# A two-layer decoder on one core: which side of the value product stands still, and where the row transposes of the routed norm are issued

## Chip, cores and metric

The kernel runs on one core of a Trainium2 chip. The metric is the device time of one execution in microseconds; the median of the runs counts. All matrix work is in float32.

## What is computed

Eight batch entries of 256 tokens with 256 features pass through two layers; each sublayer adds to x. Cut to what matters here, the reference is:

```python
x = x + L0_attn(layernorm(x))            # 16 heads of 16, rotary, full softmax
x = x + L0_xattn(ctx, layernorm(x))      # 16 heads of 16, keys and values are halves of ctx,
                                         # a bias per key and a length mask
x = x + L0_ffn(layernorm(x))             # sinkhorn gates, 8 experts, top tokens per expert
x = x + L1_attn(layernorm(x))            # 16 heads of 16, rotary, causal softmax
x = x + L1_xattn(layernorm(x), ctx)      # 16 heads of 64, one null key and value, layernorm
x = x + L1_ffn(layernorm(x))             # shared and routed experts, one expert per token
# one attention of heads of 16:
attn = softmax(einsum('bhqd,bhkd->bhqk', q, k) / 4)
out  = einsum('bhqk,bhkd->bhqd', attn, v)
```

The change touches the three attentions with heads of 16, and one step of the loop over the attention with heads of 64.

## The kernel before, in words

**Units.** The heads of 16 are worked in 24 units, one for each batch entry and attention: layer 0 takes two entries at a time (two `SelfAttention` units, then two `CrossAttention` units), then come eight causal `SelfAttention` units of layer 1. The loop at L850 runs the units in turn. While unit n is in its `core` (the generator `attention`, L315), the generator `beside(n)` (L820) gives out pieces of `end` of unit n-1 and of `prepare` of unit n+1, spread over the seven yields of the core; `experts_at` adds pieces of the layer 0 experts (`chosen_experts`, L627), which run for two entries at a time. The order of instructions on each engine is drawn up by the tile scheduler from this order and from its own estimate of when operands are ready; nothing in this stage is pinned.

**One attention.** `scores(grp)` (L324) makes, for four heads and each of two key tiles, the transposed scores `st` (keys on partitions, queries along the free side) in one of two PSUM buffers; ScalarE's exp (L343) writes them to `pT`; in the causal layer GpSimd sets the masked part to zero (L346), and the second key tile has only its 128 later queries. `values(grp)` (L360) then multiplies: the values `v_pad`, 2 heads padded to 32 columns each, stand still (64 stationary columns), and the exps of one head move (256 columns, or 128). So `o`, one PSUM buffer, holds the result with heads on partitions; the padding of ones in column 16 (`padded_values`, L289) gives the sum of the exps with it. There are four groups of four heads; after the second and the fourth group `o` is copied to `oT` by VectorE and by ScalarE (L387).

**Rows.** `end` (L482, L554) calls `rows_of` (L390): eight TensorE transposes (`oR`, L396) bring `oT` back to tokens on partitions, two reciprocals (L400) and four products (L402) on VectorE divide by the sums and write `att`. In self-attention `att` is transposed (L283) and multiplied by the output weights (`ao`, L494); in cross-attention it is added to x.

**Values.** `put_values` (L297) writes the values of a token tile into the padded buffer with two copies, on ScalarE in self-attention and on GpSimd in cross-attention. There are two padded buffers, one for even and one for odd entries, set up at the start with zeros and ones (L293, L294).

**Heads of 64.** `null_cross_attention` (L1057) loops over the entries b. In an iteration the heads of entry b are weighted (`stx` L1226, `ox` L1264, `den` L1240), entry b+1 gets its layernorm (`tr<-ident,xn`) and its projections k7, v7 and q7 (each in seven block products, `seven`, L1126), and entry b-1 gets the norm and transposes for the routed experts (`routed_norm` L958, `routed_rows` L968, on the page `tr<-ident,xne` at L283). `routed_norm`'s `xn` and layernorm_T's `xn` share one SBUF buffer. From L1379 on the instructions of TensorE are pinned to the order in which they are written, up to `order.close()` (L1407); `routed_rows` at L1377 comes just ahead of that. For the last entry, b = 7, the order is pinned at L1375, ahead of it.

**Products in two halves.** `product` (L272) issues each product as two, for 64 stationary columns each. In the profile each float32 product shows as two weight loads and two multiplies.

Of the kernel before, what the change touches and what calls it, by code (L numbers as in the profile page):

```python
# [28 lines left out]
F32 = mybir.dt.float32  # L29
# [9 lines left out]
P = 128  # L39
# [116 lines left out]
def plain(  # L156
# [139 lines left out]

    def put_values(engine_copy, v_pad, t, v):  # L297

        for g in range(2):
            engine_copy(  # L300
                v_pad[:, t, :, 3 * g, :HD].rearrange("p (c m) d -> p c m d", c=2),
                v.rearrange("p (c g m d) -> p g c m d", c=2, g=2, m=4)[:, g],
            )

    def masked_queries(work, ps, masks):

# [5 lines left out]
                nc.vector.tensor_scalar(qm[:, m], ps, masks[:, m : m + 1], None, ALU.mult)  # L312
        return qm

    def attention(kT, qm, v_pad, scale, causal, bias):  # L315

        def scores(grp):  # L324
            c, mq = divmod(grp, 2)
            pTs = []
            for kt in range(2):
                q0 = P if causal and kt else 0
                n = S - q0
                st = scp.tile([P, 2, 2, S], F32, tag="sc", name="st")  # L330
                for i in range(2):
                    for g in range(2):
                        rows = slice(64 * g, 64 * g + 64)
                        nc.tensor.matmul(  # L334
                            st[:, g, i, :n],
                            kT[rows, c, bass.ts(kt, P)],
                            qm[rows, 2 * mq + i, c, q0:],
                            start=True,
                            stop=True,
                        )  # L340
                pT = work.tile([P, 2, 2, S], F32, tag="pT", name="pT", bufs=4)
                kb = {} if bias is None else {"bias": bias[:, kt : kt + 1]}
                nc.scalar.activation(pT[:, :, :, :n], st[:, :, :, :n], AF.Exp, scale=scale, **kb)  # L343
                if causal:

                    nc.gpsimd.affine_select(  # L346
                        out=pT[:, :, :, :P],
                        in_=pT[:, :, :, :P],
                        compare_op=ALU.is_ge,
                        fill=0.0,  # L350
                        base=0,
                        pattern=[[0, 2], [0, 2], [1, P]],
                        channel_multiplier=-1,
                    )
                pTs.append(pT)
            return pTs

        oT = work.tile([P, 4, S], F32, tag="oT", name="oT")

        def values(grp, pTs, o):  # L360
            c, mq = divmod(grp, 2)
            for kt in range(2):
                q0 = P if causal and kt else 0
                for g in range(2):
                    for i in range(2):
                        nc.tensor.matmul(  # L366
                            o[64 * i : 64 * i + 64, mq, q0:],
                            v_pad[:, kt, 4 * c + 2 * mq + i, 2 * g : 2 * g + 2, :],
                            pTs[kt][:, g, i, : S - q0],
                            start=kt == 0 and g == 0,  # L370
                            stop=kt == 1 and g == 1,
                            skip_group_check=True,
                        )


        ahead = scores(0)
        yield
        for grp in range(4):
            now = ahead
            if grp % 2 == 0:  # L380
                o = op.tile([P, 2, S], F32, tag="o", name="o")
            if grp + 1 < 4:
                ahead = scores(grp + 1)
                yield
            values(grp, now, o)
            if grp % 2:
                (nc.vector.tensor_copy if grp == 1 else nc.scalar.copy)(oT[:, grp - 1 : grp + 1, :], o)  # L387
            yield oT

    def rows_of(oT, dens):  # L390

# [45 lines left out]
    class SelfAttention:  # L437
# [38 lines left out]
            yield  # L476

        def core(self):
            for self.oT in attention(self.kT, self.qm, self.v_pad, 1.0 / math.sqrt(HD), self.layer == 1, None):
                yield  # L480

        def end(self):  # L482
            b = self.b
            att = rows_of(self.oT, dens[:, 2 * self.layer, 2 * b : 2 * b + 2])
            yield
            attT = transposed(att, work, mm, "xnT")
            yield
            for t in range(2):
                xt = x[:, 2 * b + t, :]
                if self.bias is not None:  # L490
                    nc.gpsimd.tensor_tensor(xt, xt, self.bias[1], ALU.add)
                ps = mm.tile([P, 2 * D], F32, tag="mm", name="ao")[:, :D]
                for c in range(2):
                    product(ps, attT[:, c, bass.ts(t, P)], self.wo[:, c, :], c == 0, c == 1)  # L494
                nc.vector.tensor_tensor(xt, xt, ps, ALU.add)
            yield
# [27 lines left out]
    class CrossAttention:  # L524
# [23 lines left out]
            yield  # L548

        def core(self):  # L550
            for self.oT in attention(self.kT, self.qm, self.v_pad, HD**-0.5, False, kbias[:, self.b, :]):
                yield

        def end(self):  # L554
            b = self.b
            att = rows_of(self.oT, dens[:, 1, 2 * b : 2 * b + 2])
            for t in range(2):
                nc.gpsimd.tensor_tensor(x[:, 2 * b + t, :], x[:, 2 * b + t, :], att[:, t, :], ALU.add)
            yield

    first = ExitStack()
    pads = first.enter_context(tc.tile_pool(name="pads", bufs=1))
    padv = [padded_values(pads, f"padv{i}", engine) for i, engine in enumerate((nc.vector, nc.gpsimd))]
    work = first.enter_context(tc.tile_pool(name="aw", bufs=2))
    banks = ExitStack()
    mm = banks.enter_context(tc.tile_pool(name="amm", bufs=3, space=PSUM))
# [177 lines left out]
            yield  # L744


    units = []
    for b in range(0, B, 2):
        for i in range(2):
            units.append(SelfAttention(b + i, 0, wqkv0, wo0, (turned, offset), padv[i]))  # L750
        for i in range(2):
            units.append(CrossAttention(b + i, padv[i]))
    wqkv1, wo1 = weights("l1_wqkv", 3 * D, None), weights("l1_wo", D, None)
    sin1 = const.tile([P, 2, HD], F32, name="sin1")
    for b in range(B):
        units.append(SelfAttention(b, 1, wqkv1, wo1, None, padv[b % 2]))

    nc8 = XH // 2

# [297 lines left out]
    def null_cross_attention(phase):  # L1057
# [301 lines left out]
        for b in range(B):  # L1359
# [8 lines left out]
            else:  # L1368
# [4 lines left out]
                load_shared(late)  # L1373
                routing_tables(late)
                order.enter_context(tc.manual_schedule(engines={mybir.EngineType.PE}))  # L1375
            if b:
                routed_rows(b - 1, routed_norm(b - 1, work), work)  # L1377
            if more:
                order.enter_context(tc.manual_schedule(engines={mybir.EngineType.PE}))  # L1379
                kT, v, qT = key_room(), value_room(), query_room()  # L1380
                k7 = seven("k7", of_ctx, w_terms(kv_blocks, 0), kT, False)
                v7 = seven("v7", of_ctx, w_terms(kv_blocks, 1), v, True)
                q7 = seven("q7", of_x, w_terms(q_blocks, 0), qT, False)
                next(k7)
                rest()
# [1252 lines left out]
```

## Times and profile before

| what | value |
|---|---|
| median of three runs | 1373.66 us (1373.61 to 1374.96) |
| the profiled execution's own time | 1378.17 us |
| its span, first to last instruction | 1376.4 us |
| instructions | 30783 |
| mean granted TensorE clock | 0.996 |
| TensorE idle before an instruction, longest | 8.2 us (first layernorm), 2.6 and 2.4 us (`qkr`) |
| value products L366 | 1536 multiplies, 103.1 us of weight loads beside them |
| transposes of `oT`, L396 | 192 |
| reciprocal L400 / product L402 / copy L387 on VectorE, each | 248 / 281 / 690 ns |
| copy of `o` on ScalarE (L387) / copy into the padded values, each | 586 / 269 ns |
| exp of 128x1024, each | 1022 ns, with the key bias 1114 ns |

A row of the profile names the line, the engine, the operation, the result and its operands, then the shapes as partitions x elements (for TensorE: stationary rows * columns, then the moving side), the count, the busy time and the mean duration of one, and at the end the idle time of the engine just before such instructions with what ended it. PE is TensorE's multiply, PEld its weight load. In a timeline a row begins with the start and the length of a run of like instructions. Runs on PE overlap in it, because the end of one multiply lies behind the start of the next; the distance from start to start is what a run costs.

### The profile page before, as it was taken

To read this page: it belongs to the slowest core of one execution; us is meant where nothing else is said; L and a number is where in the kernel's file an instruction comes from. 1 tells how busy PE (TensorE), PEld (TensorE's weight loads), DVE (VectorE), ACT (ScalarE), POOL (GpSimd) and SP (SyncE) were. 2 spreads that over 40 slices of the span, in tenths; PEclk is the share of its full clock that TensorE was granted. 3 is DMA by queue.
4 is the path that set the end of the run, shared out by engine and by line. 5 is a ranking of instruction groups with operands and counts; after the bars stand their busy time and mean duration, and the time that the engine had idled before them with its cause. 6 is when DMAs were issued, how large, how long until landed. Compare 5 with 4: busy or idle time off the path is not lost.

```text
span 1376.4 us, 30783 instructions
## 1 busy us (share of the span) xinstructions
PE 1336.3 (97%) x13150; PEld 928.6 (67%) x13150; DVE 546.7 (40%) x1592; ACT 474.4 (34%) x758; POOL 384.3 (28%) x485
## 2 busy tenths in 40 slices
PE   6999999999999999999999999999999999999997
PEld 3666756756766756665767676777767645788874
DVE  5444463563475555344333333233222336322213
ACT  2455444443543433431322323142332312132220
POOL 4322052052033243320324323142432422300003
PEclk9999999999999999999999999999999999999999
DMA  8960000000000005000101010201101111599943
GB/s 306 343 225 16 9 25 9 9 24 2 1 9 1 2 10 183 27 1 16 31 18 33 17 32 17 48 20 29 33 16 33 64 32 63 237 372 400 402 159 120
DMA packets 46929, 116.69 MB, mean 85 GB/s; under 512 B 8272, under 2 KB 30400, under 8 KB 42432
## 3 DMA queue, kind: packets, MB, share of 16 engines
q1 hardware_dynamic: 38912, 92.74, 19.8%
q0 software_dynamic: 5152, 18.89, 3.8%
q10 hardware_dynamic: 2720, 3.02, 0.6%
q8 instruction: 105, 1.72, 0.5%
q14 instruction: 40, 0.33, 0.1%
HBM read 104.00 MB, written 27.93 MB: 96 GB/s over the span
## 4 chain that ended last, share of the span: by engine, by line
PE 81%; DMA 6%; DVE 5%; POOL 4%; issue 1%; ACT 1%; SPq 1%; ACTq 0%; POOLq 0%; DVEq 0%
PE st L334 8%; PE o L366 8%; PE v L274 6%; PE h L274 6%; PE k L274 6%; PE wo L274 5%; PE ox L1264 4%; PE stx L1226 4%; PE out L1626 3%; PE out L1443 3%; PE h L952 3%; PE tr L283 3%; PE qk L274 3%; PE hx L952 3%; PE q L274 2%; PE den L1240 2%
## 5 line engine op out<-in xcount | busy, mean ns | idle before, releaser
L366 PE MATMUL o<-pT,padv 128*64 128x256 f32 (+1 forms) x1536 | 171.6, 365 | 1.1 <-POOL pT L346 1.1
L343 ACT ACTIVATE pT<-st 128x1024 f32<-128x1024 f32 (+1 forms) x128 | 110.6, 916 | 88.1 <-PE st L334 87.3
L366 PEld LDWEIGHTS o<-pT,padv 128*64 128x64 f32 x1536 | 103.1, 137 | 52.8 <-issue 10.2
L334 PE MATMUL st<-qm,kT 64*128 64x256 f32 (+1 forms) x1024 | 116.6, 366 | 0.8 <-DVE qm L312 0.6
L334 PEld LDWEIGHTS st<-qm,kT 64*128 64x128 f32 x1024 | 89.4, 188 | 25.9 <-issue 15.6
L1232 POOL TENSOR_TENSOR both<-pTx 128x512 f32<-128x512 f32 x64 | 79.7, 1273 | 46.4 <-ACT pTx L1230 38.9
L274 PE MATMUL h<-xrT,w 128*64 128x128 f32 (+1 forms) x1936 | 87.2, 250 | 0.0
L274 PEld LDWEIGHTS h<-xrT,w 128*64 128x64 f32 x1936 | 84.7, 137 | 2.8 <-ACT yr L1635 1.0
L343 ACT ACTIVATE pT<-st,kbias 128x1024 f32<-128x1024 f32 x64 | 68.0, 1113 | 28.7 <-PE st L334 28.7
L1230 ACT ACTIVATE pTx<-stx 128x1024 f32<-128x1024 f32 x64 | 62.2, 1022 | 41.7 <-PE stx L1226 39.8
L256 POOL TENSOR_TENSOR lnrs<-lnve,mhalf 128x2 f32<-128x2 f32 x48 | 33.7, 704 | 147.5 <-DVE lnve L254 94.4
L334 PE MATMUL st<-qm,memk 64*128 64x256 f32 x512 | 68.8, 393 | 0.5
L945 DVE TENSOR_TENSOR midr<-sl,h 128x128 f32<-128x128 f32 x102 | 29.4, 288 | 100.4 <-PE h L274 67.2
L944 ACT ACTIVATE sl<-h 128x128 f32<-128x128 f32 (+1 forms) x114 | 35.4, 310 | 97.8 <-PE h L274 55.3
L1226 PE MATMUL stx<-qTx,kTx 64*128 64x256 f32 x512 | 64.3, 391 | 2.5 <-ACT pTx L1230 2.5
L274 PE MATMUL qk<-l_wqkv,xnT 128*64 128x512 f32 x256 | 63.0, 613 | 0.7 <-ACT xnT L286 0.7
L346 POOL TENSOR_SCALAR_AFFINE_SELECT pT<-pT 128x512 f32<-128x512 f32 x64 | 40.0, 646 | 81.9 <-ACT pT L343 78.7
L1264 PE MATMUL ox<-pTx,vx 128*64 128x256 f32 x512 | 61.1, 381 | 0.0
L1226 PEld LDWEIGHTS stx<-qTx,kTx 64*128 64x128 f32 x512 | 46.1, 186 | 20.3 <-ACT pTx L1230 7.2
L334 PEld LDWEIGHTS st<-qm,memk 64*128 64x128 f32 x512 | 48.0, 186 | 15.1 <-issue 5.1
L274 PE MATMUL wo<-wout_x,oT 128*64 128x256 f32 x512 | 58.0, 379 | 0.0
L1315 POOL TENSOR_TENSOR oT<-oT,rs 128x512 f32<-128x512 f32 x30 | 37.3, 1275 | 64.8 <-DMA rs<-rd 64.8
(341 smaller groups left out, 2289.5 us busy)
## 6 DMA issues: line engine op xcount, KB each, us to landing
w<-packs SPq DMA_DIRECT2D x22, 1408.0 KB
w<-packs SPq DMA_DIRECT2D x22, 768.0 KB
rs<-rd SPq DMA_DIRECT2D x16, 512.0 KB
packs<-L_ffn_w_eDF SPq DMA_DIRECT2D x8, 704.0 KB
packs<-L_ffn_w_eDF SPq DMA_DIRECT2D x8, 640.0 KB
packs<-L_ffn_w_eFD SPq DMA_DIRECT2D x8, 640.0 KB
ctxT<-ctx_T SPq DMA_DIRECT2D x8, 512.0 KB
wkv_x<-L_xattn_Wkv POOLq DMA_DIRECT2D x1, 4096.0 KB
```

Source lines behind the costliest of these rows:

```text
L274: nc.tensor.matmul(out[h], lhsT[:, h], rhs, start=start, stop=stop, skip_group_check=True)
L283: nc.tensor.transpose(ps[:, c, t * P : (t + 1) * P], rows[:, t, c * P : (c + 1) * P], ident)
L334: nc.tensor.matmul(st[:, g, i, :n], kT[rows, c, bass.ts(kt, P)], qm[rows, 2 * mq + i, c, q0:], start=True, stop=True,)
L343: nc.scalar.activation(pT[:, :, :, :n], st[:, :, :, :n], AF.Exp, scale=scale, **kb)
L366: nc.tensor.matmul(o[64 * i : 64 * i + 64, mq, q0:], v_pad[:, kt, 4 * c + 2 * mq + i, 2 * g : 2 * g + 2, :], pTs[kt][:, g, i, : S - q0], s ...
L952: nc.tensor.matmul(h, shared["ws13"][:, c, lo : lo + P], shared["xnT"][:, c, bass.ts(q, 2 * S)], start=c == 0, stop=c == 1)
L1226: nc.tensor.matmul(st[:, g, kt, :], kT[rows, c, bass.ts(kt, P)], qT[rows, c, :], start=True, stop=True)
L1230: nc.scalar.activation(pT, st, AF.Exp, scale=scale)
L1232: nc.gpsimd.tensor_tensor(both, pT[:, :, 0, :], pT[:, :, 1, :], ALU.add)
L1264: nc.tensor.matmul(o[XD * g : XD * (g + 1), i, :], v[:, kt, 2 * (c2 + i) + g, :], pT[:, g, kt, :], start=kt == 0, stop=kt == 1, skip_group ...
L1443: nc.tensor.matmul(ps, mid[:, i, lo : lo + P], w2[:, i, :], start=i == 0, stop=i == NFC - 1)
L1626: nc.tensor.matmul(ps[h], mid[:, i, h], sets[k % len(sets)][1][:, i, :], start=i == 0, stop=i == NFC - 1, skip_group_check=True,)
```

## The change

It has two parts.

**Exp stands still.** For entries from the third on (b of 2 and more in layer 0) and for all of layer 1, the values lie in new buffers `valv` of 17 columns a head (16 values and a one), and `attention` sees this from the shape. `turned_values` takes the exps of 64 queries as the stationary side (64 columns) and the 17 columns of one head as the moving side. The result has queries on partitions: `o` is 2 token tiles x 8 heads x 17. `weighted` then takes the reciprocals of column 16 and multiplies straight from PSUM into `att`, on VectorE, after the second and fourth group. No `oT` and no `rows_of` are made for these units; `end` finds `att` ready. `put_values` needs one copy a token tile instead of two. Entries 0 and 1 of layer 0 keep the old form.

**Pinned rows.** In the loop over the entries of the attention with heads of 64, the pinned order of TensorE starts ahead of `routed_rows` instead of after it, for b of 1 to 6 (for b = 0 there is no such call).

```diff
     def put_values(engine_copy, v_pad, t, v):
+        if len(v_pad.shape) == 4:
+            engine_copy(v_pad[:, t, :, :HD], v.rearrange("p (h d) -> p h d", d=HD))
+            return
         for g in range(2):
...
+    def values_and_ones(pool, name, engine):
+        t = pool.tile([P, 2, H, HD + 1], F32, name=name)
+        engine.memset(t[:, :, :, HD:], 1.0)
+        return t
...
-    def attention(kT, qm, v_pad, scale, causal, bias):
+    def attention(kT, qm, v_pad, scale, causal, bias, dens):
...
-        oT = work.tile([P, 4, S], F32, tag="oT", name="oT")
+        turned = len(v_pad.shape) == 4
+        if turned:
+            att = work.tile([P, 2, D], F32, tag="att", name="att")
+        else:
+            oT = work.tile([P, 4, S], F32, tag="oT", name="oT")
+
+        def turned_values(grp, pTs, o):
+            c, mq = divmod(grp, 2)
+            for g in range(2):
+                for i in range(2):
+                    head = 4 * g + 2 * mq + i
+                    for t in range(2):
+                        kts = 1 if causal and t == 0 else 2
+                        for kt in range(kts):
+                            for h in range(2):
+                                q = t * P + 64 * h - (P if causal and kt else 0)
+                                nc.tensor.matmul(
+                                    o[64 * h : 64 * h + 64, t, head, :],
+                                    pTs[kt][:, g, i, q : q + 64],
+                                    v_pad[:, kt, 8 * c + head, :],
+                                    start=kt == 0,
+                                    stop=kt == kts - 1,
+                                    skip_group_check=True,
+                                )
+
+        def weighted(c, o):
+            r = dens[:, :, 8 * c : 8 * c + 8]
+            nc.vector.reciprocal(r, o[:, :, :, HD])
+            nc.vector.tensor_tensor(
+                att[:, :, c * P : (c + 1) * P].rearrange("p t (h d) -> p t h d", d=HD),
+                o[:, :, :, :HD],
+                r.unsqueeze(3).to_broadcast([P, 2, 8, HD]),
+                ALU.mult,
+            )
...
             if grp % 2 == 0:
-                o = op.tile([P, 2, S], F32, tag="o", name="o")
+                o = op.tile([P, 2, 8, HD + 1] if turned else [P, 2, S], F32, tag="o", name="o")
...
-            values(grp, now, o)
+            (turned_values if turned else values)(grp, now, o)
             if grp % 2:
-                (nc.vector.tensor_copy if grp == 1 else nc.scalar.copy)(oT[:, grp - 1 : grp + 1, :], o)
-            yield oT
+                if turned:
+                    weighted(grp // 2, o)
+                else:
+                    (nc.vector.tensor_copy if grp == 1 else nc.scalar.copy)(oT[:, grp - 1 : grp + 1, :], o)
+            yield (lambda: att) if turned else lambda: rows_of(oT, dens)
...
         def end(self):
             b = self.b
-            att = rows_of(self.oT, dens[:, 2 * self.layer, 2 * b : 2 * b + 2])
+            att = self.rows()
             yield
...
+    valv = [values_and_ones(pads, f"valv{i}", engine) for i, engine in enumerate((nc.vector, nc.gpsimd))]
...
     for b in range(0, B, 2):
+        padv = padv if b < 2 else valv
...
-        units.append(SelfAttention(b, 1, wqkv1, wo1, None, padv[b % 2]))
+        units.append(SelfAttention(b, 1, wqkv1, wo1, None, valv[b % 2]))
...
+            if more:
+                order.enter_context(tc.manual_schedule(engines={mybir.EngineType.PE}))
             if b:
                 routed_rows(b - 1, routed_norm(b - 1, work), work)
             if more:
-                order.enter_context(tc.manual_schedule(engines={mybir.EngineType.PE}))
                 kT, v, qT = key_room(), value_room(), query_room()
```

## The prediction

> **What bounds the kernel now.** I read the page first (busy shares and the chain), then the PE groups kept apart by shape, then the PE timeline of single stretches, and last the waits of PE.
>
> ```profile
> span 1376.4 us, 30783 instructions
> ...
> PE 1336.3 (97%) x13150; PEld 928.6 (67%) x13150; DVE 546.7 (40%) x1592; ACT 474.4 (34%) x758; POOL 384.3 (28%) x485
> ...
> PE 81%; DMA 6%; DVE 5%; POOL 4%; issue 1%; ACT 1%; SPq 1%; ACTq 0%; POOLq 0%; DVEq 0%
> ```
>
> TensorE sets the time: 97% busy, 81% of the chain. In the waits of PE the whole run holds some 33 us of idle, 8.2 of it the start; between 60 and 660 us, where the changed units lie, it is under 12 us. So the change is priced on PE, by start-to-start distances in its timeline, because a busy sum counts the 0.2 us end of a pipelined run twice.
>
> ```profile
> L366 PE MATMUL o<-pT,padv 128*64 128x256 f32 x1280 | 157.8, 384 | 1.1 <-POOL pT L346 1.1
> ...
> L396 PE MATMUL oR<-ident,oT 128*128 128x128 f32 x192 | 27.1, 280 | 0.5 <-ACT oT L387 0.4
> ...
> L366 PE MATMUL o<-pT,padv 128*64 128x128 f32 x256 | 19.8, 273 | 0.0
> ```
>
> Each float32 product shows as two load-and-multiply pairs. L366 is the value product (64 stationary columns, 256 or 128 moving); L396 turns its result back into rows, 8 transposes in each of 24 units. The next fence has the nearest rows to the new shape: `lg` (8 moving columns) and `cs` (16), both with 64 stationary columns that alternate between the two halves of the output, exactly the order of the new loop.
>
> ```profile
> 144.16 1.95 PE L274 MATMUL ao<-l_wo,xnT 128*64 128x256 f32 x16
> 145.94 0.59 PE L274 MATMUL lg<-gate,xnT 128*64 128x8 f32 x16
> 146.37 1.93 PE L366 MATMUL o<-pT,padv 128*64 128x256 f32 x16
> 148.13 0.36 PE L274 MATMUL cs<-g,ones 128*64 128x16 f32 x8
> 148.42 2.00 PE L334 MATMUL st<-qm,kT 64*128 64x256 f32 x16
> ```
>
> 16 pairs of `lg` take 146.37 - 145.94 = 0.43 us: **26.9 ns a pair**. `cs` between two stages of its own kind (272.48 to 272.68, 8 pairs) takes 25.0. The longest run of such pairs, `h` with 64 moving columns (1214.17 to 1219.31, 176 pairs), takes 29.2.
>
> [...]a 16-instruction L366 group takes 1.76 us before a stage of its own mode and 1.86 before a transpose (139.79 to 141.65), so a change costs some 0.1 us here.
>
> **The change, part by part.** 20 of the 24 units change: 12 in layer 0 (256 queries against two key tiles, 4 groups each: 48 groups) and 8 causal ones (32 groups).
>
> *Transposes out of rows_of.* 8 per unit, as here:
>
> ```profile
> 548.19 1.52 PE L366 MATMUL o<-pT,padv 128*64 128x256 f32 x16
> 549.64 1.58 PE L334 MATMUL st<-qm,kT 64*128 64x256 f32 x16
> 551.15 1.09 PE L396 MATMUL oR<-ident,oT 128*128 128x128 f32 x8
> 552.25 1.58 PE L334 MATMUL st<-qm,kT 64*128 64x256 f32 x16
> ```
>
> 1.10 us here, 1.02 at 262.59, 0.93 at 135.33: mean 1.04, times 20 = **-20.8 us**.
>
> *The value product.* Old, pure stream: 16 instructions in 1.73 us (205.80 to 207.53, 108 ns each); causal, 8 of these and 8 at 54.5 (`h` at 128 columns: 4.85 us for 88, rounded down) = 1.30. Sum 48 x 1.73 + 32 x 1.30 = 124.6 us. New: 32 products, 64 pairs a group, causal 24 and 48: 48 x 64 + 32 x 48 = 4608 pairs. **Break-even is 27.0 ns a pair**; each ns more costs 4.6 us. The bounds are 25.0 (4608 x 0.025 = 115.2: -9.4) and 29.2 (134.6: +10.0). I take 27.5, just over `lg`, because a group is four times as long as `lg`'s run: 126.7, **+2.1 us**. Mode changes at the ends stay as they are.
>
> *The row work.* DVE loses a 0.69 us copy, two 0.25 reciprocals and four 0.28 products per unit (2.3 us) and gets two reciprocals at 0.25 and two products of 256 elements, estimated at 0.48 from the row of `ys` (L736): 1.5. ACT loses a 0.59 copy and, in self-attention, half of its four 0.27 copies into padv; POOL likewise. All of it lies beside PE: nothing gained. What is late next: `o` has one buffer, so the next value product waits for `weighted` (0.73 us, against 0.69 for the old copy), and a score stage of 1.5 to 1.9 us covers that. Without this cover it would be 0.8 us twice a unit. The last unit has no cover: values end at 614.55, transposes of att start at 616.45 over copy, oR, reciprocal and product; now 0.9 us. **-1.0 us.** The two extra memsets of ones (0.09 and 0.14 us by L294) lie in the 8.2 us wait for the input.
>
> *A stall that the transposes covered.* At 549.64 to 553.75 oR parts two score stages. The score buffers are two, so the second stage may not begin before the first exp is done: where two such stages meet elsewhere (stx at 959.32) exp starts 1.24 us in and takes 0.97, and the second stage starts at 2.31 instead of 1.93. In the causal units the stage is only 1.51 long: a stall of 2.25 - 1.51 = 0.74 at most. Upper end 8 x 0.74 + 12 x 0.3 = 9.5 us, lower end 0, since the att transposes (ready by then) can move into the gap. I take 0.1 a unit: **+2.0 us**. The stationary side is now pT, so a whole group needs both exps at its first head, where the old loop needed the second halfway; a score stage lies in between, counted in the same bounds.
>
> *Rows in the pinned order.* For b of 1 to 6 the four xne transposes come before k7's first product instead of inside it:
>
> ```profile
> 977.42 0.66 PE L283 MATMUL tr<-ident,xn 128*128 128x128 f32 x4
> 978.00 0.87 PE L274 MATMUL k<-ctxT,wkv_x 128*64 128x128 f32 x10
> 978.81 0.44 PE L283 MATMUL tr<-ident,xne 128*128 128x128 f32 x2
> 979.17 0.44 PE L274 MATMUL k<-ctxT,wkv_x 128*64 128x128 f32 x4
> ```
>
> That saves three or four mode changes. But xne shares a buffer with xn, so DVE makes it only after PE has read xn: at 978.19 to 978.92, behind a copy of oT that ends at 978.2. The transposes can then end at about 979.2, and k's 31 instructions at 54.5 ns end at 981.0; they now end at 980.84. Queued behind the wait are all of k7, v7 and q7, and the exps of the next entry behind those. +0.15 x 6 = **+0.9 us**; from -0.6 x 6 = -3.6, if DVE makes xne before that copy, to +0.6 x 6 = +3.6, if no mode change is saved.
>
> **Sum.** -20.8 + 2.1 - 1.0 + 2.0 + 0.9 = -16.8 us. The profiled execution took 1378.2 (span 1376.4 and 1.8 around it), so 1361.4 profiled. The runs' median, 1373.66, lies 4.5 under the profiled one: **1356.9**.
>
> **Rivals.** (A) *The pair pitch is longer than lg's.* Place: the 80 changed value groups. It decides from 124.6 + 16.8 + 2.1 = 143.5 us, 31 ns a pair. For it: `sc`, also 8 columns, needs 0.55 us for 16 (1017.49 to 1018.04), 34.4 ns, and no run as long with 17 columns is in the trace; the instruction stream of a group grows fourfold. Against it: 176 pairs at 29.2. At 34.4: 158.5 - 124.6 = +33.9 in place of +2.1: 1388.7, slower. (B) *The gap closes but PE waits.* The transposes were filler; the full score stall (+7.5 over my value) and one more stall like that at 303 (2.44 us, after which y took 3.41 instead of 1.97: the granted clock was 0.72 from 306 to 312[...]) give 7.5 + 3.9: 1368.3. For it: waits of 2.6 and 2.4 us on qkr exist. Against it: stx waited only 2.5 us in all. (C) *Pitch of 30.5 to 31:* +14 to +16 more than my value, 1371 to 1373, no change.
>
> **Numbers.** The forecast's case 0.72, B 0.14, C 0.05, A 0.09. About 0.2% (2.7 us) is what a measurement of this kernel can tell from no change. The pitch bounds alone give 1345.4 to 1364.8; with the stall's upper end, up to B, 1345 to 1368.5, which leaves out A, C and little else. Faster 0.86, same 0.05, slower 0.09.
>
> **What would show it.** Value groups of 64 pairs that follow each other at 1.7 to 1.9 us (causal 1.3 to 1.4); 32 of 192 oR instructions left; PE idle from 60 to 660 us not over 15 us; xne transposes in one run of four after xn's, with a wait of about 0.6 us on DVE. Groups of 2.1 us or more would mean A; a row of waits of st on pT would mean B.

## Result and the profile after

| | before | after |
|---|---|---|
| median | 1374.31 us (1373.61 to 1376.04, 4 runs) | **1391.47 us** (1384.71 to 1397.77, 4 runs) |
| ratio, 95% interval | | **1.0113** [1.0089, 1.0138] |
| span of the profiled execution | 1376.4 us | 1385.7 us |
| first product after the changed stage (`fm`, L274) starts at | 621.1 us | 629.4 us |

The forecast was 1356.9 us, faster; the changed kernel is 17 us slower. The page of the changed kernel, in the order in which I read the one before:

```profile
span 1385.7 us, 36933 instructions
...
PE 1332.5 (96%) x16318; PEld 954.8 (69%) x16318; DVE 528.8 (38%) x1533; ACT 461.7 (33%) x710; POOL 381.3 (28%) x474
...
PE 66%; issue 2%; DVE 2%; POOL 1%; ACT 1%; DMA 1%; SPq 0%; ACTq 0%; POOLq 0%
...
L385 PE MATMUL o<-valv,pT 128*64 128x17 f32 x4608 | 147.3, 210 | 2.4 <-POOL pT L357 2.4
```

TensorE is as busy as before. The new product has the 4608 pairs that were counted on. The transposes went too: 32 of 192 `oR` instructions are left.

```profile
L443 PE MATMUL oR<-ident,oT x32: 272/273/328, 50.8 to 113.2; 128*128 128x128 f32 x32
```

The loss lies in the attention stage (8.3 of the 9.3 us by which the spans differ); an iteration of the loop over the heads of 64 went from 60.61 to 60.73 us. So I looked for it in the timeline of PE. Here it is from 231 us on (start, length of the run, line, operation, shapes, count):

```profile
231.23 1.03 PE L274 MATMUL v<-l_wqkv,xnT 128*64 128x256 f32 x8
232.19 2.00 PE L345 MATMUL st<-qm,kT 64*128 64x256 f32 x16
234.12 0.66 PE L283 MATMUL tr<-ident,qkr 128*128 128x128 f32 x4
234.62 0.60 PE L521 MATMUL qps<-ident,qkr 128*128 128x128 f32 x4
235.15 3.97 PE L385 MATMUL o<-valv,pT 128*64 128x17 f32 x128
239.04 3.58 PE L345 MATMUL st<-qm,kT 64*128 64x256 f32 x16
242.55 0.66 PE L283 MATMUL tr<-ident,xnb 128*128 128x128 f32 x4
243.14 2.00 PE L345 MATMUL st<-qm,kT 64*128 64x256 f32 x16
```

Three score stages `st`, of the same 16 instructions. Those at 232.19 and 243.14 take 1.93 us from start to start; the one at 239.04 takes 3.51. No wait stands ahead of it: no row carries an idle time in brackets. What differs is what ran just before, 128 pairs with 17 moving columns. The same stretch in windows (third column of numbers: the granted clock of TensorE):

```profile
228.00:235.00 7.00, 7.00 (x98) 1.00 0.00 0
235.00:238.50 3.50, 3.50 (x118) 1.00 0.02 5
238.90:242.30 3.40, 3.40 (x22) 0.50 0.26 82
242.30:249.30 7.00, 7.00 (x118) 1.00 0.00 0
```

PE was busy in every microsecond, and still the clock went to half from 238.86 to 242.27, 3.41 us. The execution has three more falls in this stage, at 505, 604 and 624.5 us; these follow waits of 2.2, 2.1 and 1.5 us (the last in two parts, 0.82 and 0.68). So neither waits nor groups of few columns stand ahead of every fall (see "Open" below). The page's `PEclk` row shows none of it: its 40 slices are 35 us long. The waits of PE grew as well; these are the ones that were absent or shorter before (us in total, times, longest):

```profile
PE st L345 <- ACT pT L354: 6.7, 10, 2.1
...
PE cps L737 <- DMA by_half<-slots: 2.8, 2, 2.0
...
PE cs L274 <- DVE g L707: 2.5, 7, 0.8
PE o L385 <- POOL pT L357: 2.4, 2, 2.2
```

To keep the parts apart I use a **ledger of the stage** from 60 us to the start of `fm`, one profiled execution for each kernel. *Clock lost* is the sum over windows of 1 us of (1 - granted clock); *idle* is PE's; *rest* is what remains (an idle microsecond at half clock is taken off twice, a small amount). *Changes* counts, in the order in which TensorE's multiplies start, from the first one to `fm`, how often the rows and columns of the stationary side change (64*128 for scores, 128*128 for transposes, 128*32 for experts, 128*64 for most others).

| kernel | moving columns | changes | `fm` starts | clock lost | idle | rest |
|---|---|---|---|---|---|---|
| before | 256 | 296 | 621.1 | 1.7 | 13.0 | 546.4 |
| after | 17 | 308 | 629.4 | 6.8 | 21.5 | 541.1 |
| values_only | 17 | 308 | 641.5 | 25.6 | 17.5 | 538.4 |
| layer1_only | 17 in layer 1 | 300 | 635.7 | 13.6 | 18.5 | 543.6 |
| no_transposes | 256 | 282 | 606.6 | 0.0 | 17.9 | 528.7 |
| before_late | 256 | 360 | 638.7 | 1.7 | 14.6 | 562.4 |
| late | 17 | 332 | 634.2 | 15.6 | 15.2 | 543.4 |
| late_wide32 | 32 | 318 | 617.0 | 3.4 | 12.8 | 540.8 |
| wide20 | 20 | 311 | 636.1 | 13.7 | 21.3 | 541.1 |
| wide24 | 24 | 308 | 620.2 | 3.4 | 16.9 | 539.9 |
| wide28 | 28 | 284 | 624.1 | 8.6 | 21.2 | 534.3 |
| wide32 | 32 | 282 | 613.0 | 3.4 | 16.0 | 533.6 |
| pinned17 | 17 | 266 | 643.2 | 32.7 | 26.4 | 524.1 |
| pinned24 | 24 | 267 | 625.5 | 10.2 | 26.3 | 529.0 |
| pinned32 | 32 | 267 | 623.2 | 10.2 | 25.0 | 528.0 |
| pinned_before | 256 | 286 | 627.6 | 6.8 | 20.5 | 540.3 |

Some expectations below name counts of changes that differ from these (289, 291 and 293); the table has those of the traces.

The profiled execution of after was one of its quicker ones. Over its four runs (clock 0.990, 0.979, 0.982, 0.991) the time times (1 - clock) is 20.2 us on average; over the 18 runs of before that were timed beside wide24 it is 7.9.

### The profile page after: what moved, and what is told of

It reads as the page before. It is cut to its first block, busy times and chain, and to the rows that moved or that the text cites. A ratio compares the mean times of both kernels' runs of the same rounds, so it can differ in the third digit from the quotient of the medians.

```text
span 1385.7 us, 36933 instructions
## 1 busy us (share of the span) xinstructions
PE 1332.5 (96%) x16318; PEld 954.8 (69%) x16318; DVE 528.8 (38%) x1533; ACT 461.7 (33%) x710; POOL 381.3 (28%) x474
## 4 chain that ended last, share of the span: by engine, by line
PE 66%; issue 2%; DVE 2%; POOL 1%; ACT 1%; DMA 1%; SPq 0%; ACTq 0%; POOLq 0%
PE h L274 6%; PE v L274 5%; PE k L274 5%; PE o L385 5%; PE st L345 4%; PE ox L1316 4%; PE wo L274 4%; PE stx L1278 4%; PE out L1679 3%; PE out L1496 3%; PE h L1004 3%; PE hx L1004 3%; PE q L274 2%; PE den L1292 2%; PE qk L274 2%
## 5 line engine op out<-in xcount | busy, mean ns | idle before, releaser
L385 PEld LDWEIGHTS o<-valv,pT 128*64 128x64 f32 x4608 | 141.5, 138 | 13.9 <-issue 8.7
L385 PE MATMUL o<-valv,pT 128*64 128x17 f32 x4608 | 147.3, 210 | 2.4 <-POOL pT L357 2.4
L345 PE MATMUL st<-qm,kT 64*128 64x256 f32 (+1 forms) x1024 | 121.6, 373 | 5.5 <-ACT pT L354 5.0
L345 PEld LDWEIGHTS st<-qm,kT 64*128 64x128 f32 x1024 | 92.7, 192 | 29.2 <-issue 12.5
L274 PE MATMUL h<-xrT,w 128*64 128x128 f32 (+1 forms) x1936 | 87.3, 250 | 3.9 <-issue 3.9
L274 PEld LDWEIGHTS h<-xrT,w 128*64 128x64 f32 x1936 | 84.7, 137 | 6.8 <-issue 4.6
L345 PE MATMUL st<-qm,memk 64*128 64x256 f32 x512 | 72.3, 396 | 1.9 <-ACT pT L354 1.7
L997 DVE TENSOR_TENSOR midr<-sl,h 128x128 f32<-128x128 f32 x102 | 29.4, 288 | 104.9 <-PE h L274 70.3
L274 PE MATMUL qk<-l_wqkv,xnT 128*64 128x512 f32 x256 | 63.2, 616 | 0.7 <-ACT xnT L286 0.7
L274 PE MATMUL wo<-wout_x,oT 128*64 128x256 f32 x512 | 58.0, 379 | 0.0
```

What stands on the lines that cost most here:

```text
L274: nc.tensor.matmul(out[h], lhsT[:, h], rhs, start=start, stop=stop, skip_group_check=True)
L345: nc.tensor.matmul(st[:, g, i, :n], kT[rows, c, bass.ts(kt, P)], qm[rows, 2 * mq + i, c, q0:], start=True, stop=True,)
L385: nc.tensor.matmul(o[64 * h : 64 * h + 64, t, head, :], pTs[kt][:, g, i, q : q + 64], v_pad[:, kt, 8 * c + head, :], start=kt == 0, stop=k ...
```

## The experiments

Two theories, guesses of mine to be tested. **G**: the granted clock goes by how much streams through the array, not by whether PE is busy; long stretches of products with few columns bring half clock with no wait at all. **W** (the rival): only waits lower the clock, so the loss is the score stall and its like. Later a third joined, **O**: the order that the scheduler draws up.

**1. The product alone.** At the end of the kernel before, stretches of 640 pairs with 64 stationary columns in alternating halves, between full-length products; then 320 pairs with 128 stationary columns.

```python
for i in range(count):
    for h in range(P // m):
        nc.tensor.matmul(ps[m * h : m * h + m, ...], x[:, i % NT, m * h : m * h + m], x[:, i % NT, D - n :], ...)
```

> The kernel before, with six runs of products put in between the attention with heads of 64 and the experts, nothing else changed; the results of the added products are not used. Each run is parted from the next by 48 products with 512 moving columns. 640 pairs each with 64 stationary columns and 17, 32, 64 and 8 moving ones, then 320 pairs each with 128 stationary columns and 17 and 64 moving ones. Theory G [...]: in the 17 and 8 column runs the granted clock falls to 0.5 after at most 7 us and stays there to the end of the run (pitch then 29 growing to 45 or more ns), in the 64 column run it stays at 1.0; 32 shows on which side of the threshold it lies. Theory W (only waits of TensorE lower the clock): the clock is 1.0 in all runs. Pitch: if the issue of the pair is the limit, 17, 32 and 64 columns all give 29 to 30 ns and 8 too; if lg's 26.9 ns was the true value for few columns, 8 and 17 give 27 and 64 gives 29.

Windows of the stretches: 17 columns (cut where the clock falls), 32, 64, 8, then 128 stationary columns with 17 and with 64 moving.

```profile
1173.04:1179.30 6.26, 6.26 (x218) 1.00 0.02 5
1179.30:1201.89 22.59, 22.59 (x430) 0.50 0.01 2
1224.89:1243.52 18.63, 18.63 (x642) 1.00 0.02 4
1264.15:1282.82 18.67, 18.67 (x643) 1.00 0.02 4
1303.42:1332.83 29.41, 29.41 (x642) 0.60 0.01 3
1355.31:1419.21 63.90, 63.90 (x322) 0.54 0.00 1
1442.88:1478.75 35.87, 35.87 (x322) 1.00 0.00 1
```

Nothing waits anywhere here. With 17 columns the full clock lasts 6.3 us and then it is half to the end: 640 pairs take 28.85 us. With 32 or 64 columns the same number takes 18.63 and 18.67 us, 29.1 ns a pair, at full clock throughout. So more work in the same instructions is quicker. With 8 columns the clock falls too (0.60 in the mean), and with 128 stationary columns it falls for 17 moving ones (0.54) and not for 64 (1.00). The half clock without a wait that G expected is there; W's "only waits" does not hold in a bare stretch.

**2. What the pair pitch is, and from how many columns on.**

> As the first probe, with other runs: 640 pairs with 64 stationary columns that alternate between the halves and 20, 24 and 28 moving columns; 320 pairs with 40 moving columns all in one half; 640 pairs with 48 moving columns and the order 0, 0, 1, 1 of the halves. The results of the added products are not used. Theory G: the threshold lies between 17 columns (clock 0.5 in the first probe) and 32 (clock 1.0), so at least one of the three shows the fall and those above it none. Pitch: if two weight loads of 64 columns go on at once, one in each half, the one-half run takes twice the pitch, 56 to 59 ns, and 0, 0, 1, 1 lies between 29 and 58; if the issue of instructions were the limit, all of them would take 29 ns.

20, 24 and 28 columns: 18.64 us for 640 each, the time of 32 columns at full clock (18.63). That none of the three loses the clock was not expected: in a bare stretch of 640 pairs 17 columns lost it and 20 kept it. One half alone, 40 columns: 319 pairs in 18.53 us, **58.1 ns** a pair. Halves in the order 0, 0, 1, 1: 29.1 ns again. So load and multiply take 58.1 ns in one half and, with both halves in turn, half of that: 58.1 / 2 = 29.1, as if the two halves went on side by side. At full clock the pitch stays at 29 ns from 17 to 64 moving columns and is 112 ns with 128 stationary ones (35.87 us for 320): in these runs it goes by the stationary columns and their halves, and not by the moving columns or the number of instructions. `lg` has the same pitch: in its run the starts come in twos, 6 or 7 ns apart, and from two to two it is 58.4 ns, 29.2 a pair. Only the first step from two to two is shorter (28 ns), and over 16 pairs that gives 26.9.

**3 and 4. One part of the change alone.** values_only is after with the pinned order at its old place; pin_only is before with the pinned order moved.

```diff
+            if more:
+                order.enter_context(tc.manual_schedule(engines={mybir.EngineType.PE}))
             if b:
                 routed_rows(b - 1, routed_norm(b - 1, work), work)
             if more:
-                order.enter_context(tc.manual_schedule(engines={mybir.EngineType.PE}))
```

> The changed kernel with the pinned order starting where it did before; only the exps stand still. Both theories: the pinned rows cost 0.1 us in each of six iterations, so 0.5 to 1 us faster than the changed kernel with the same clock; against the kernel before still slower by 0.5 to 1.5%. A time below 1374 us would mean that the pinned rows are the loss.

> The kernel before with only the pinned order moved ahead of routed_rows. Both theories: +0.6 to +1 us against the kernel before (0.1 to 0.15 in each of six iterations), no change in the granted clock; a wait of about 0.6 us on xne's transposes in each iteration.

values_only 1392.61 us against 1377.84, ratio 1.0093 [1.0073, 1.0114]; pin_only 1378.96, ratio 1.0000 [0.9988, 1.0012]. The loss comes with the first part of the change; the pinned rows make no difference that these runs can show. In values_only's profiled execution 25.6 us of clock are lost, in after's 6.8, though TensorE has the same instructions in the same order up to `fm`: the loss is large and changes from execution to execution. Five of the seven falls in values_only's stage (37.5 of its 51.2 us at half clock) have no wait of 0.3 us or more in the 10 us ahead of them. Here is the first one, and the stretch ahead of it:

```profile
155.70:165.90 10.20, 10.20 (x58) 0.50 0.09 27
145.00:155.60 10.60, 10.39 (x256) 1.00 0.01 2
```

**5. More columns, the same instructions.** After, with 32 moving columns: 17 of the head and 15 of its neighbour, whose results nobody reads.

```diff
-                                    v_pad[:, kt, 8 * c + head, :],
+                                    flat_of[id(v_pad)][:, 17 * (16 * kt + 8 * c + head) : 17 * (16 * kt + 8 * c + head) + 32],
...
-                o = op.tile([P, 2, 8, HD + 1] if turned else [P, 2, S], F32, tag="o", name="o")
+                o = op.tile([P, 2, 8, 32] if turned else [P, 2, S], F32, tag="o", name="o")
```

> The changed kernel, but 32 columns move instead of 17: the 17 of the head and the first 15 of its neighbour, whose products land in unused columns of the result. The number of instructions is the same. Theory G: more streams through the array in the value groups (the profile's value group of 64 pairs keeps 1.88 us[...]), the lost clock shrinks and so does the spread of the runs: 1378 to 1385 us. Theory W: the clock and the spread stay as they were (1385 to 1398 us) or the time grows with the columns.

1373.16 us, ratio **0.9963** [0.9950, 0.9976]: quicker than both kernels, and quicker than G's range. The waits that W blames are still there (same columns):

```profile
PE st L350 <- ACT pT L359: 6.8, 10, 2.2
...
PE cs L274 <- DVE g L712: 2.6, 7, 0.6
```

6.8 us in 10 waits of `st`, as in after (6.7 in 10). W falls as the main cause of the lost clock. But not all of this gain is the clock: over its six runs 12.4 us are lost to it, against 20.2 in after, so 7.8 us of the 18 between the two kernels (see 13 to 18).

**6 to 8. Another order.** If long unbroken stretches of value pairs were the trouble, the fourth value group of a unit could go behind the first score stage of the next unit; this would also cover the score stall. late has it with 17 columns, late_wide32 with 32, before_late is the kernel before with it.

```diff
-        for i, _ in enumerate(u.core()):
+        core = u.core()
+        for i in range(7):
+            next(core)
+            if i == 0 and tail is not None:
+                for _ in tail:
+                    pass
...
+        tail = core
+        next(experts_at, None)
```

> The changed kernel (17 columns), but the fourth value group of a unit is issued after the first score stage of the next unit, so that no two value groups follow each other and the score stages have a value group between them. Theory G: no run of value products is longer than 2 us, [...]the clock returns to 0.993 to 0.997, the spread of the runs to that of the kernel before, and the waits of st on pT (6.5 us) fall under 2 us: 1362 to 1372 us. Theory W with the waits alone as the cause: the waits fall too, and the clock with them, but then the 128-pair runs would be innocent, and the widened kernel's clock could not have risen with its waits unchanged.

> The same order with 32 moving columns. Theory G: 1361 to 1370 us; at most 3 us below the 17 columns, since the clock has little left to recover. If the 17 columns lose clock in this order as well, the difference is 5 us or more.

> The kernel before (values stand still, 256 columns move) with this order of the fourth value group. Theory G: its runs of value products stream all the time, so the order gains nothing there by the clock; the score stages had the transposes between them: within 0.3% of the kernel before. If the order by itself is worth 6 us or more, the gain of the late kernel is not due to the clock and the covered stalls of the turned form.

late: 1392.25 us, ratio 1.0129 [1.0106, 1.0152], expectation missed. The clock still falls, at 183, 285 and 371 to 388 us among others, so parting the last two groups of a unit is not enough. late_wide32: 1370.52, ratio 0.9965 [0.9952, 0.9978]: the waits of `st` on `pT` go from 6.8 to 2.0 us, and the time stays, since the rest grows by 7.2. It is 21.7 us quicker than late, and over the runs late loses 17.4 us more to the clock (24.8 and 7.4). before_late: 1391.26, ratio 1.0120 [1.0099, 1.0141], expectation missed too, and the ledger says why: no more clock lost, hardly more idle, but 64 more changes of tile kind and 16.0 us more rest, by estimate **0.25 us a change** (16.0 / 64). The kernels of the table in which all 20 units are turned agree with it: from 266 to 332 changes their rest grows by 0.27 us a change (a straight line through the eleven). I had priced a change at 0.1.

**9. 20 columns in the kernel.**

> The changed kernel with 20 moving columns instead of 17. In the bounds probe 20 columns kept the full clock and 17 lost it, at the same 29.1 ns a pair. Theory G: the full gain of the 32 columns is there already, 1370 to 1376 us, 0.2 to 0.5% under the kernel before[...]. Theory W: as the changed kernel, 1385 us or more.

1395.3 us, ratio 1.0125 [1.0107, 1.0143], missed, with 23.4 us of clock lost over the runs: 20 columns keep the clock in a bare stretch but not here, where transposes, small products and waits lie between the groups.

**10. No transposes, old product.** Before, without the 20 x 8 transposes: `att` is made of the rows of `oT` as they lie and a constant in place of the sums' reciprocals.

```diff
-            for k in range(4):
-                nc.tensor.transpose(ps[:, k, :], oT[:, k, bass.ts(t, P)], ident)
...
+            if through:
...
+            else:
+                rows = oT.rearrange("p k s -> p (k s)")[:, 4 * P * t : 4 * P * (t + 1)].rearrange("p (n w) -> p n w", w=HP)
```

> The kernel before without the eight row transposes in 20 of the 24 units: the products of the row step read oT itself and a constant in place of the reciprocals, so this attention is left out of the result but for its timing. Nothing else changes, and the exps still move. Theory G with the covered stall: the 20.8 us of the transposes come off PE, 3 to 8 us come back as waits of st on pT and of the small chains, the clock stays at 0.994 or more: 1357 to 1366 us. If the whole 20.8 us are gained, 1354 to 1356, the transposes covered nothing and the waits of the changed kernel come from its value product.

1362.57 us against 1379.55, ratio 0.9888 [0.9868, 0.9908], 15.4 us less by the ratio. The stall appears here as well, without a turned product:

```profile
PE st L335 <- ACT pT L344: 6.8, 7, 1.6
```

So the transposes did cover a score stall, and of the 21 us in them some 5 come back as waits (idle 17.9 against 13.0).

**11. Only layer 1 turned.**

```diff
-        padv = padv if b < 2 else valv
```

> The changed kernel with the exps standing still in layer 1 alone (17 columns); layer 0 keeps the old form throughout. Theory G: in layer 1 the runs are 48 pairs (1.4 us) with products of 512 and 256 columns between most of them, so little clock is lost there (at most 4 us); 8 units times 1.04 for the transposes against 8 x 4 x 0.09 for the pitch and up to 0.9 a unit for the stall: -6 to +4, 1369 to 1379 us, and most of the changed kernel's loss is in layer 0. If it is 1384 us or more, layer 1 carries the loss.

1390.64 us, ratio 1.0081 [1.0059, 1.0102], missed. The 8 causal units alone bring most of the loss. Its falls of the clock at 507 and 610 us follow waits of 3.0 us (`o` on the masked `pT`) and 2.1 us (`st` on `pT`); the longest, from 473 to 484 us, has only waits of 0.8 and 0.2 us ahead of it, among groups of 17 columns.

**12. The last wait of wide32.** Its clock falls once more at 587 us, after a wait of 2.2 us in the last unit. wide32_tables makes the tables of the null key after that unit's core.

> The 32-column kernel, and the tables for the null key made after the last unit's core instead of before it, so that their products of 3.6 us lie in the last unit's end chain (waits of 0.8, 0.7 and 0.9 us, and the half clock after them) and their use of pT's buffers no longer holds up that unit's exps (2.2 us). Both theories: 3 to 6 us under the 32-column kernel, 1364 to 1370 us, 0.6 to 0.9% under the kernel before.

1373.34 us, ratio 0.9955 [0.9938, 0.9973], not told apart from wide32's; the expected 3 to 6 us aren't there. The idle went to `nvw` (3.0 us), and the clock falls at 603 instead.

**13 and 14. 24 and 28 columns.**

> The changed kernel with 24 moving columns instead of 17 (7 of the neighbour's, whose results nobody reads). 20 columns still lost the clock in the kernel and 32 did not. [...]the value groups with 24 columns stand between: a ratio to the kernel before between 0.997 and 1.010 and lost clock of 4 to 10 us. If there is a threshold in the kernel just over 20, it is as good as 32: 0.9963 within 0.002, lost clock about 3 us. If the gain with 32 columns came from something else than the streamed amount, 24 is like 20 and 17: 1.011 to 1.013.

> As with 24, with 28 moving columns. Streamed amount: as good as 32 or nearly, 0.996 to 0.999, lost clock 3 to 5 us. Something that belongs to 32 alone: 1.008 or more.

wide24 1382.31 us against 1377.25, ratio 1.0040 [1.0019, 1.0061]; wide28 1376.89, ratio 0.9998 [0.9987, 1.0009]. With 17, 20, 24, 28 and 32 columns the ratios are 1.0113, 1.0125, 1.0040, 0.9998, 0.9963: graded. But wide28 loses as much clock over its runs as wide24 (13.1 and 11.8 us on average; 3 to 5 were expected) and is 5 us quicker, so something else moves along. The order shows it: with 17, 20 and 24 columns there are 308 to 311 changes, with 28 and 32 columns 284 and 282. Only the number of moving columns and the room for them were edited, so the scheduler must have gone by it, presumably through its estimate of how long an instruction takes. Experiment 5 had not held the order fixed.

**15 to 18. One order for all.** TensorE pinned to the written order through all 24 units. With 17, 24 and 32 columns its instructions then stand in the same order up to `fm` (in the trace of 17 columns one transpose in the last unit has another place).

```diff
+    pinned = ExitStack()
+    pinned.enter_context(tc.manual_schedule(engines={mybir.EngineType.PE}))
     for n, u in enumerate(units):
...
+    pinned.close()
```

> The changed kernel with TensorE's instructions of the attention stage (all 24 units) held to the order in which they are written, so that the order no longer hangs on the scheduler's estimates of how long 17 or 32 columns take. If the missing streamed columns cost the clock and the clock is the main loss, this one is slower than the same order with 32 columns by 10 us or more. If most of the difference between 17 and 32 columns was the order (the 32-column kernel has 282 changes of kind among its TensorE runs, the changed kernel 293), this one and the 32-column one lie within 4 us of each other. Against the kernel before: 1.004 to 1.015 by the clock, 0.994 to 0.999 by the order.

> The same order with 24 moving columns. By the clock: between the two others. By the order: equal to both within 3 us.

> The same order with 32 moving columns; written order has 267 changes of kind instead of 282. [...]more waits, since the written order doesn't know what is ready: 0.990 to 1.000 of the kernel before.

> The kernel before with its attention stage in the written order too, to see what the written order does without the change. It has 289 changes of kind instead of 291: 0.995 to 1.010 of the kernel before. If it lies below 0.995, part of what a pinned changed kernel gains is the written order and not the change.

| kernel | median | ratio to before (1377.29 us) | mean clock over the runs |
|---|---|---|---|
| pinned17 | 1397.34 us | 1.0129 [1.0100, 1.0158] | 0.975 |
| pinned24 | 1384.17 us | 1.0049 [1.0032, 1.0065] | 0.984 |
| pinned32 | 1381.31 us | 1.0035 [1.0022, 1.0048] | 0.988 |
| pinned_before | 1383.42 us | 1.0041 [1.0028, 1.0054] | 0.991 |

With one order, 17 columns in place of 32 cost 16.0 us by the medians. In the profiled executions `fm` starts 20.0 us later (643.2 and 623.2), and the clock lost differs by 22.5 (32.7 and 10.2); over all runs it differs by 17.8 (34.7 and 16.9). With instructions, order and waits alike, only the moving columns are left to explain it: G holds as far as these runs go. The two timelines from 150 us on, first pinned17:

```profile
150.88 2.02 PE L385 MATMUL o<-valv,pT 128*64 128x17 f32 x64
153.23 0.41 PE L274 MATMUL cs<-g,ones 128*64 128x16 f32 x8 [0.33 <-DVE g L707]
153.46 2.70 PE L385 MATMUL o<-valv,pT 128*64 128x17 f32 x64
155.94 0.65 PE L274 MATMUL cs<-g,ones 128*64 128x16 f32 x8
156.51 3.79 PE L345 MATMUL st<-qm,memk 64*128 64x256 f32 x16
```

and pinned32, the same five runs:

```profile
151.55 2.04 PE L390 MATMUL o<-valv,pT 128*64 128x32 f32 x64
153.91 0.41 PE L274 MATMUL cs<-g,ones 128*64 128x16 f32 x8 [0.32 <-DVE g L712]
154.13 2.07 PE L390 MATMUL o<-valv,pT 128*64 128x32 f32 x64
156.00 0.42 PE L274 MATMUL cs<-g,ones 128*64 128x16 f32 x8
156.35 2.00 PE L350 MATMUL st<-qm,memk 64*128 64x256 f32 x16
```

The same wait (0.33 and 0.32 us), the same instructions; but the second value group takes 2.48 us instead of 1.87 and the score stage doubles. Windows of 150 to 162 us, pinned17 and then pinned32:

```profile
150.00:162.00 12.00, 11.67 (x188) 0.72 0.08 25
```

```profile
150.00:162.00 12.00, 11.61 (x228) 1.00 0.08 25
```

The order counts too. pinned17 to pinned32 have the lowest rest of all (524.1 to 529.0), but the most idle (25 to 26 us): the written order doesn't know what is ready. pinned32 was expected at 0.990 to 1.000 and missed that. But pinned_before is slower than before, so a pinned kernel is to be held against that one: 1381.31 against 1383.42 us. wide32 stays among the quickest, with late_wide32 and wide32_tables.

## Why the prediction was wrong, step by step

**Transposes, -20.8: right.** The start-to-start sum of `oR` from 110 us to the end of the stage went from 23.6 to 1.0 us; 1.4 of it was idle, so -21.2. (The three distances of the prediction have the mean 1.02 and not 1.04.)

**The value product, +2.1: the step that failed.** Its size, in a layer 0 group with the same stage behind it, before and after:

```profile
287.91 1.95 PE L366 MATMUL o<-pT,padv 128*64 128x256 f32 x16
289.68 1.89 PE L274 MATMUL qk<-l_wqkv,xnT 128*64 128x512 f32 x8
```

```profile
192.60 2.05 PE L385 MATMUL o<-valv,pT 128*64 128x17 f32 x64
194.48 1.92 PE L274 MATMUL qk<-l_wqkv,xnT 128*64 128x512 f32 x8
```

A group of 64 pairs takes 1.88 us, 29.4 ns a pair and not 27.5, against 1.77 for the old one; a causal group takes 1.42 (541.96 to 543.38) against 1.36 (537.47 to 538.83). 48 x 0.11 + 32 x 0.06 = 7.2; all distances of `o` from 115 us on, less idle and half clock, went from 131.9 to 139.3, **+7.4**. Both sides of the sum were off. The old price of 1.73 came from the row at 205.80, which is `back`, of the same shapes but not a value product. And I had taken the price of a pair from `lg`, whose 26.9 ns hold one short step (28 ns in place of 58.4) in so few pairs; the longer runs of probe_bounds gave 58.1 ns in one half and 29.1 in halves by turns. Nor was 25.0 a lower bound: `cs`'s 25.0 has the same short first step as `lg`'s 26.9 (29 and 28 ns), and single starts lie 6 or 7 ns apart. The bound that I had from the long run of `h`, 29.2, was the better neighbour.

More than its size, its **frame** was wrong: I priced the product by its pitch alone, with the clock held at 1, and brought the clock in only under rival B, behind waits. The traces show the clock at 0.50 for 3.41 us or a multiple of it, and not behind waits alone: in probe_pitch 17 columns every 29 ns leave PE at 100% busy, and after 6.3 us the clock falls. Over the runs this is 20.2 - 7.9 = **+12.3 us**, which no step of mine had.

**Score stall and other waits, +2.0:** idle in the stage rose by **8.5** (21.5 - 13.0). The sign, the place (`st` on `pT`, 6.7 us in 10 waits) and the upper end of 9.5 were right, the value taken was not. The limit of 15 us idle from 60 to 660 us was exceeded (21.5; before had 13.3 there, not under 12).

**Order, not in the sum.** Transposes and product should have changed the rest by -21.2 + 7.4 = -13.8. In wide32 they nearly do (533.6 - 546.4 = -12.8). In after it is -5.3: **+8.5 us** come back. Much of it lies in the score stages, whose distances, less idle and half clock, are 142.6 us before, 148.2 in after and 143.0 in wide32. no_transposes went from 296 to 282 changes of kind when the transposes left, and wide32 has 282 too; after has 308. At 0.25 us a change the 26 are 6.5 of the 7.5 us between after and wide32. That "mode changes at the ends stay as they are" was an assumption that I hadn't tested.

**Row work, -1.0:** not seen; in the last unit `tr` still waits 0.8 us for `att`.

**Pinned rows, +0.9: right.** The loop's period grew by 0.12 us where I had 0.15, 0.7 us for six; pin_only's 0.0 us is too coarse to show it. The picture was right; four `xne` transposes in one run, behind a wait of 0.67 us (put down to ScalarE's copy here, not to VectorE):

```profile
986.50 0.66 PE L283 MATMUL tr<-ident,xn 128*128 128x128 f32 x4
987.82 0.67 PE L283 MATMUL tr<-ident,xne 128*128 128x128 f32 x4 [0.67 <-ACT xnT L286]
```

**The balance.** From -16.8 predicted to +17.2 measured are 34.0 us: clock 12.3, order 8.5, waits 6.5, product 5.3, row work 1.0, less 0.4 for the transposes and 0.2 for the pinned rows: 33.0. The terms of the ledger come from one execution and the clock from means over runs, so agreement to 2 us is as much as can be asked. The clock is the largest term and turned the change into a loss; but the gain was gone without it. Time times clock is 1370.0 us for values_only and 1370.4 for before in the same session.

**Rivals.** A had the right sign and the wrong reason: its pitch of 34.4 never came at full clock. B named both waits and the half clock, and the waits that were to show it, of `st` on `pT`, came; but it tied the clock to idle time and was priced as a gain. In its own example a wait of 2.44 us ended at 305.49 us and the clock was half from 306.07 to 309.48, 3.41 us.

**Open.** What the granted clock goes by. The clock records of the traces narrow it down. From 30 us to `fm` all stretches at half clock inside a run begin a whole number of 3.41 us apart (238.86 to 505.10 us in after is 78.0 of them). Whether that is why runs of one kernel differ by 13 us was not shown.

For each window of 3.41 us at full clock, I added up how long moving columns streamed, at 0.42 ns a column (a 512-column product of probe_pitch takes 215 ns). This is an estimate over all kernels and probes here, without the first 15 us of each. Of 72 windows with less than 23% streaming, 70 were followed by half clock; of 93 with 23 to 30%, 23; of 167 with 30 to 39%, 14; of 7614 with more, none. A bare stretch of pairs has 24% with 17 columns, 29% with 20 and 46% with 32. Between 115 us and `fm`, before has 2 windows under 39%, after 24 and wide32 4. By this estimate waits and few columns would count alike; but it does not part the windows sharply (23 of 93, 14 of 167), and what the clock goes by stays open. So does how much of 28 to 32 columns (5 us by the ratios, at 284 and 282 changes) is clock and how much the detail of two slightly different orders.

## What to carry to other kernels

Before you swap sides so that a short operand moves, ask how much of each pair's time the moving columns will stream (by the estimate above 24% with 17 columns, 46% with 32): at 29 ns a pair, 17 columns lost the clock and 32 columns, at the same pitch, mostly kept it, so padding the moving side cost nothing and gained 16 us in a fixed order. (With the padding and the scheduler's order the change is worth 0.4% against before.) Price such products by a stretch of some ten microseconds and not by the nearest short row, and look at the clock in windows of a few microseconds, since the page's slices hide its falls. A removed stage can also take its cover and the scheduler's order with it (without the transposes idle went from 13.0 to 17.9 us and the changes from 296 to 282): count the waits and the tile changes afterwards.

## What was new about the hardware

TensorE went to half clock with no idle time at all, in after for 3.41 us from 238.86 us on; in a bare stretch 640 pairs with 17 moving columns took 28.85 us, with 32 or 64 columns 18.63 and 18.67. Pairs of load and multiply with 64 stationary columns took 58.1 ns each in one half and 29.1 in alternating halves, also in the order 0, 0, 1, 1. And a change of tile kind in this stage cost, by estimate, nearer 0.25 us (16.0 us for 64 of them) than the 0.1 that a single place showed.
